# Decoder layer stack on one core: odd heads' sums taken from the exponentials, cross scores in two steps, a new order of work

## The chip, the cores and the metric

The kernel runs on one core of a Trainium2 chip, in one launch. The metric is the device time of that core in microseconds, as a median over runs. The core has five engines that run side by side: PE (TensorE, the matrix products and transpositions), DVE (VectorE), ACT (ScalarE, which computes the exponentials), POOL (GpSimd) and SP (SyncE, which here only issues transfers). They meet at semaphores. PE writes its results into PSUM, in banks of 128 x 512 numbers, and PE cannot reuse a bank before ACT or DVE has read it.

## What is computed

There are 4 sequences of 512 tokens with 128 channels. Three blocks follow each other, each with a residual sum and a layer norm: a retention attention with 16 heads, a cross attention to 32 keys for each sequence, and a stack of six layers of local attention (16 heads of 64, windows of 32 that look at themselves and the window before) and a gated FFN. Cut to what matters here:

```python
def local_attention(q, k, v):
    ...
    sim = jnp.einsum('bhwie,bhwje->bhwij', bq, bk2) * QK_SCALE
    sim = jnp.where(mask, -jnp.finfo(sim.dtype).max, sim)
    attn = jax.nn.softmax(sim, -1)
    out = jnp.einsum('bhwij,bhwje->bhwie', attn, bv2)
...
def _L0_xattn_ref(key, value, query, mask, inv_scale_factor, W1, b1, W2, b2, W3):
    q = jnp.einsum('bqd,hd->bqh', query, W1) + b1
    k = jnp.einsum('bkd,hd->bkh', key, W2) + b2
    qk = jnp.einsum('bqh,bkh->bqk', q, k) / inv_scale_factor
    attn = jax.nn.softmax(qk, axis=-1)
...
for i in range(DEPTH):      # 6
    x = attn_layer(shift_tokens(x), Wqkv[i], q_scale[i], k_scale[i], Wo[i]) + x
    x = ffn_layer(shift_tokens(x), ln_g[i], ln_b[i], W1[i], b1[i], W2[i], b2[i]) + x
```

## The kernel before

**An order written out ahead.** The kernel first records all its work as steps and only then emits it. A step (`Step`, recorded by `Work.do` at line 328) belongs to one engine and has a planned cost in us, a function that issues its instructions, the slots that it reads and writes, and a priority. A slot is a tile to be: a place in an SBUF pool or a PSUM bank. `Plan.order` (line 180) plays the steps through: an engine that is free takes, among the waiting steps that find room for their slots, the one with the lowest priority; on PE it may pass over up to `KEEP` = 4.5 units of priority to avoid a dear turn from one kind of work to another (`TURN`, `TURNS`, lines 143 to 148). A step is over after its planned cost; those that read from it may start `LAG` = 0.25 us later, and the slots that it was last to use are free again at its planned end (lines 228 to 232). The list that comes out is the order of instructions on every engine, SP's transfers too. The chip then runs each engine in exactly this order, with semaphores wherever one engine needs another. The planned costs thus never appear as times on the chip; they only decide who stands before whom.

A priority is a base (the number of the unit of work), an offset, and a correction from the table `SHIFT` (lines 294 to 317), whose keys are a group letter and the number of the step in its group: P for a pair of heads of the first block, X for cross attention, u for a unit of the layers, q for its values, f for the FFN, w, v, k for weights. `ROOM` (line 286) says how many places each slot kind has: three PSUM banks `mm`, two `tr`, two `so`, one `f`; a bank asked for as `mm` may also come from the other pools.

**Front.** Lines 394 to 1030: for each sequence eight pairs of heads (`pair`), then `finish` (residual, norm) and `cross`. `cross` (line 977) makes the scores of a sequence in one step on PE (`scores`, lines 987 to 992): for each of four blocks of 128 tokens a product of x with the folded keys and a product of a row of ones with the bias row, both added up in PSUM. One DVE step then takes the maximum, ACT the exponentials, DVE the shares.

**Layers.** For each layer, sequence, half of the heads (8) and block of 128 tokens there is a unit: 6 x 4 x 2 x 4 = 192 of them (`unit`, line 1209, and `attend`, line 1335). A unit has these steps, by the lines that the profile shows:

- PE: two projections pq and pk, each a product of three passes (`mm3`, lines 87 to 89)
- ACT: squares sq (1258). DVE: rotary products t1 and t2 (1242, 1251), norms (1275, 1282). POOL: their sum (1264)
- ACT and POOL: inverse norms r, u (1345 to 1352); POOL scales t1 by r (1362)
- PE: transpositions ptq and ptk (96). ACT: copies into qT and kT (1385). POOL: the window before (1397)
- PE: scores of 8 heads (1408, 1421), even heads into the bank s0, odd heads into s1
- DVE: maxima mx of both (1441), and even heads' scores minus maximum (1450)
- ACT: for the odd heads four exponentials of 64 columns each, with the maximum as bias (`exps`, 1460); for the even heads one exponential over all four (1463)
- DVE: sums su of all 8 heads (1466) and their inverse (1467). POOL: weights times inverse sums (1473)
- PE: transposition pp (1483). ACT: copy pT (1487)
- PE: output O of 32 small products (1499), which also needs the values vb

Every two units share the values: four products pv (PE), four copies v (ACT, 1306), and twelve transfers on SP that lay v out by windows in vb (1313 to 1325). vb has two places, so its transfers wait until O of two pairs before has read it. After the four blocks of both halves come `add_attention` (1510) and `ffn` (1534), whose second product is pyf (1625).

The matters around the change: the bank s1 goes to the exponentials in `exps` and is free after them; `su` has three places; `total` (lines 1465 to 1469) is one DVE step of two instructions.

## Time and profile before

| | us |
|---|---|
| median of 3 runs | 2003.3 (2001.99 to 2007.96) |
| the profiled execution | 2008.77 |
| its span | 2007.1 |

The span is the time between the first and the last instruction of the profile; the 1.7 us to the execution's time lie around it. The mean granted clock of TensorE was 0.976. By the timeline, the first block and most of cross attention take the first 360 us, the first scores of a layer begin at 409.0 us and the last at 1973 us. The first O of the six layers begins at 423, 707, 969, 1229, 1486 and 1744 us.

Some groups of the layers, with the mean of one instruction as recorded:

| line, engine | instruction | count | busy us | mean ns |
|---|---|---|---|---|
| L1264 POOL | t1q, t1k sum, 128x512 | 384 | 500.0 | 1302 |
| L1362 POOL | t1q, t1k times r, 128x512 | 384 | 402.1 | 1050 |
| L1275 DVE | norms, 128x1024 | 192 | 231.8 | 1207 |
| L1306 ACT | copy v, 128x512 | 384 | 219.8 | 602 |
| L1473 POOL | weights times inverse sums, 128x512 | 192 | 204.2 | 1068 |
| L1463 ACT | even heads' exponential, 128x256 | 192 | 81.0 | 436 |
| L1450 DVE | even heads' scores minus maximum, 128x256 | 192 | 76.7 | 409 |
| L1467 DVE | inverse of the sums, 128x8 | 192 | 39.0 | 203 |
| L1586, L1587 ACT | table loads around the FFN's gelu | 25 + 25 | 64.2 | 1283 |
| L989, L990 PE | cross scores, x part and bias part, 32 columns | 32 + 32 | 14.5 | 308, 313 |

How to read it: a record lasts from the start of an instruction to its end, and the next one may start before that, on every engine. So records add up to more than the engine needs; the distance from one start to the next is the price of an instruction in a row of others. A matrix product of 32-bit numbers appears as two records. The waits of an engine name what released it last.

### The profile page before, as it was taken

How to read it: one execution, taken by the hardware profiler on the slowest of the kernel's cores; microseconds unless marked ns; L12 is line 12 of the kernel's file. 1: busy time of each engine (PE TensorE's matmuls, PEld its weight loads, DVE VectorE, ACT ScalarE, POOL GpSimd, SP SyncE). 2: the span in 40 equal slices, each digit the busy share in tenths (PEclk: the TensorE clock that was granted, in tenths of full speed). 3: DMA queues.
4: the chain of work that ended last, by engine and by line, in shares of the span. 5: the costliest groups of instructions: out<-in, count | busy, mean ns of one | idle time of the engine just before them, and what ended most of it. 6: DMA issues, size and time to landing. Idle time of an engine off the chain costs nothing.

```text
span 2007.1 us, 71083 instructions
## 1 busy us (share of the span) xinstructions
PE 1850.5 (92%) x28633; PEld 1405.3 (70%) x28633; DVE 1611.1 (80%) x3482; ACT 1587.4 (79%) x4048; POOL 1441.8 (72%) x1847
## 2 busy tenths in 40 slices
PE   7999999788898999989999999999999998999996
PEld 5676677566676777767777777777777776767675
DVE  5787786757787798886998868989788897888885
ACT  7877765689887788878888888888878897788785
POOL 3444444666777688886887878878878888787882
PEclk9999997789999999999999999999999999999999
DMA  3000001254555565665555555656655565545662
GB/s 90 1 6 2 1 2 34 67 130 109 133 148 123 131 152 139 156 150 147 133 132 146 146 146 142 166 123 160 150 142 144 125 157 149 142 107 134 146 172 60
DMA packets 146464, 233.02 MB, mean 116 GB/s; under 512 B 23770, under 2 KB 39000, under 8 KB 146136
## 3 DMA queue, kind: packets, MB, share of 16 engines
q1 hardware_dynamic: 146136, 228.46, 45.7%
q8 instruction: 228, 3.74, 0.8%
q14 instruction: 100, 0.82, 0.1%
HBM read 31.25 MB, written 2.10 MB: 17 GB/s over the span
## 4 chain that ended last, share of the span: by engine, by line
PE 57%; ACT 18%; DVE 14%; DMA 4%; issue 3%; SPq 3%; POOL 1%; DVEq 0%; ACTq 0%; POOLq 0%
PE O L1499 6%; PE s L1421 4%; PE pv L87 4%; DMA vb<-v 4%; PE pv L89 3%; PE pv L88 3%; PE ptk L96 3%; PE pp L1483 3%; PE ptq L96 2%; SPq L1325 2%; PE pyf L1625 2%; DVE nx L1275 2%; ACT sq L1258 2%; ACT v L1306 2%; PE pq L87 1%
## 5 line engine op out<-in xcount | busy, mean ns | idle before, releaser
L1264 POOL TENSOR_TENSOR t1q<-t1q,t2q 128x512 f32<-128x512 f32 x192 | 248.7, 1295 | 66.4 <-DVE t2q L1251 62.6
L1264 POOL TENSOR_TENSOR t1k<-t1k,t2k 128x512 f32<-128x512 f32 x192 | 251.3, 1310 | 55.4 <-DVE t2k L1251 40.7
L1473 POOL TENSOR_TENSOR pr<-pr,su 128x512 f32<-128x512 f32 x192 | 204.2, 1068 | 91.0 <-DVE su L1467 73.7
L1306 ACT COPY v<-pv 128x512 f32<-128x512 f32 x384 | 219.8, 602 | 42.7 <-PE pv L89 37.4
L1275 DVE TENSOR_REDUCE nx<-sq 128x16 f32<-128x1024 f32 x192 | 231.8, 1207 | 4.9 <-ACT sq L1258 3.7
L1499 PE MATMUL O<-vb,pT 128*32 128x128 f32 x6144 | 210.9, 279 | 10.5 <-DMA vb<-v 4.8
L1499 PEld LDWEIGHTS O<-vb,pT 128*32 128x32 f32 x6144 | 165.0, 111 | 63.3 <-issue 30.3
L1362 POOL TENSOR_TENSOR t1q<-t1q,r 128x512 f32<-128x512 f32 x192 | 201.2, 1051 | 2.7
L1362 POOL TENSOR_TENSOR t1k<-t1k,r 128x512 f32<-128x512 f32 x192 | 200.9, 1049 | 0.0
L1421 PE MATMUL s<-kT,qT 64*32 64x64 f32 x12288 | 169.8, 223 | 22.6 <-issue 22.5
L1460 ACT ACTIVATE pr<-s,mx 128x64 f32<-128x64 f32 x768 | 178.2, 325 | 9.8 <-DVE mx L1441 9.8
L1441 DVE TENSOR_REDUCE mx<-s 128x4 f32<-128x256 f32 x384 | 145.6, 413 | 42.7 <-PE s L1421 41.3
L1242 DVE TENSOR_TENSOR t1k<-pk,tl 128x512 f32<-128x512 f32 x192 | 130.7, 681 | 56.0 <-PE pk L89 34.8
L1242 DVE TENSOR_TENSOR t1q<-pq,tl 128x512 f32<-128x512 f32 x192 | 130.7, 681 | 50.7 <-PE pq L89 37.0
L1421 PEld LDWEIGHTS s<-kT,qT 64*32 64x32 f32 x12288 | 151.0, 105 | 25.0 <-issue 24.5
L1258 ACT ACTIVATE sq<-pk 128x512 f32<-128x512 f32 x192 | 116.1, 610 | 41.6 <-DVE t1k L1242 23.9
L1251 DVE TENSOR_TENSOR t2q<-pq,tl 128x512 f32<-128x512 f32 x192 | 130.0, 677 | 21.0 <-ACT sq L1258 20.1
L1466 DVE TENSOR_REDUCE su<-pr 128x8 f32<-128x512 f32 x192 | 129.3, 673 | 20.8 <-ACT pr L1463 12.0
L1251 DVE TENSOR_TENSOR t2k<-pk,tl 128x512 f32<-128x512 f32 x192 | 130.4, 679 | 18.8 <-ACT sq L1258 18.6
L1487 ACT COPY pT<-pp 128x512 f32<-128x512 f32 x192 | 113.3, 596 | 24.3 <-PE pp L1483 23.1
L1258 ACT ACTIVATE sq<-pq 128x512 f32<-128x512 f32 x192 | 115.6, 614 | 20.9 <-DVE t1q L1242 18.2
L96 PE MATMUL ptq<-ident,t1q 128*128 128x128 f32 x768 | 120.0, 280 | 11.6 <-DVE t2k L1251 4.6
(1002 smaller groups left out, 5428.3 us busy)
## 6 DMA issues: line engine op xcount, KB each, us to landing
vb<-v SPq DMA_DIRECT2D x576, 256.0 KB
vb<-v SPq DMA_DIRECT2D x192, 128.0 KB
vb<-v SPq DMA_DIRECT2D x288, 64.0 KB
vb<-in_c_zero_dram SPq DMA_DIRECT2D x96, 64.0 KB
wo<-in_L_ffn_Wo_dram SPq DMA_DIRECT2D x12, 256.0 KB
tb<-in_c_tabs_dram SPq DMA_DIRECT2D x12, 256.0 KB
w1r<-in_L_ffn_W_dram SPq DMA_DIRECT2D x6, 341.0 KB
xt<-in_x_dram SPq DMA_DIRECT2D x4, 256.0 KB
```

The source lines that it names most:

```text
L96: self.nc.tensor.transpose(bank[: blk.shape[1], tslice(t)], blk, self.ident)
L1242: nc.vector.tensor_tensor(out=t1(), in0=ps().rearrange("p (h d) -> p h d", d=DH), in1=tl()[:, 2 * j, t : t + 1, :].to_broadcast([P, 8, DH] ...
L1251: nc.vector.tensor_tensor(out=t2().rearrange("p h (z d) -> p h z d", z=2), in0=ps().rearrange("p (h z d) -> p h z d", d=32, z=2)[:, :, ::- ...
L1258: do("ACT", self.A512, lambda ps=ps, j=j: nc.scalar.activation(sq()[:, j], ps(), AF.Square), [ps], [sq])
L1264: lambda t1=t1, t2=t2: nc.gpsimd.tensor_tensor(out=t1(), in0=t1(), in1=t2(), op=ALU.add),
L1275: nc.vector.tensor_reduce(out=near()[:, :, 0], in_=sq().rearrange("p j (h d) -> p (j h) d", d=DH), op=ALU.add, axis=AX.X,)
L1306: do("ACT", self.A512, lambda pv=pv, j=j, e=e: nc.scalar.copy(v()[:, j, e], pv()), [pv], [v])
L1362: lambda x=x, j=j: nc.gpsimd.tensor_tensor(out=x(), in0=x(), in1=r()[:, j].unsqueeze(2).to_broadcast([P, 8, DH]), op=ALU.mult),
L1421: nc.tensor.matmul(sv[e]()[rows, p, :], lhsT=qT()[c, p, rows], rhs=kT()[c, p, 32 * w : 32 * w + 64], start=False, stop=True, skip_group_ch ...
L1460: nc.scalar.activation(pr()[:, a, 1], sv[1]()[:, a], AF.Exp, bias=mx()[:, a, 1:2])
L1473: lambda: nc.gpsimd.tensor_tensor(out=flat(), in0=flat(), in1=su().unsqueeze(2).to_broadcast([P, 8, 64]), op=ALU.mult),
L1499: nc.tensor.matmul(o[rows, t], lhsT=pT()[:, p, rows], rhs=vb()[:, t % 2, w, tslice(p)], start=(h2 == t == p == 0), stop=(h2 == 1 and p == ...
```

## The change

Four parts. In `exps`, each of the four exponentials also delivers the sum of its 64 columns (`accum_out`) into an odd column of `su`; `total` then sums only the even heads (128 x 256 instead of 128 x 512) before it takes the inverses. In `cross`, the scores are two steps of two blocks each; a step first writes the bias for both blocks with one product and then adds the two products of x. In the plan, a slot that becomes free is given out `GIVE` = 0.2 us after the planned end of its last user instead of at once, `TURNS` has other prices, some planned costs are different, and the planned time of a weight's load is 11 us instead of 8. The table `SHIFT` has new numbers throughout, so the order of steps on all engines is another one. Nothing else of what is computed is changed.

```diff
+    GIVE = 0.2
+
     TURN = 0.04
     TURNS = {
-        ("t", "t"): 0.08, ("t", None): 0.0, (None, "t"): 0.0, ("t", "S"): 0.17, ("t", "O"): 0.17, (None, "S"): 0.09,
-        (None, "O"): 0.09, ("S", "t"): 0.17, ("S", None): 0.17, ("S", "O"): 0.27, ("S", "f"): 0.17,
-        ("O", "t"): 0.0, ("O", None): 0.0, ("O", "S"): 0.0, ("O", "f"): 0.0, ("t", "f"): 0.08,
+        ("t", "t"): 0.08, ("t", None): 0.0, (None, "t"): 0.06, ("t", "S"): 0.17, ("t", "O"): 0.17, (None, "S"): 0.12,
+        (None, "O"): 0.12, ("S", "t"): 0.2, ("S", None): 0.19, ("S", "O"): 0.19, ("S", "f"): 0.17,
+        ("O", "t"): 0.1, ("O", None): 0.1, ("O", "S"): 0.09, ("O", "f"): 0.1, ("t", "f"): 0.08, ("f", "O"): 0.2,
     }
...
+                if over == 2:
+                    for g in st.freed:
+                        free[g] += 1
+                    continue
                 busy.discard(st.eng)
+                st.freed = []
                 for s in st.slots:
                     left[s] -= 1
                     if left[s] == 0 and s.tags:
-                        free[s.got] += 1
+                        st.freed.append(s.got)
+                if st.freed:
+                    heapq.heappush(events, (now + self.GIVE, st.n, 2, st))
...
     SHIFT = dict(
-        C1=5.5, C2=8.5, C3=-2.75, D0=19.5, D2=12.75, D3=-11.25, D4=-0.5, D6=3.25, D7=12.25, D8=-1.25, D9=-7.75,
...
+        C0=-7, C2=1.5, C3=-6.75, D0=11, D1=-7.75, D2=-0.75, D4=13.5, D5=9.25, D6=1.25, D7=-11.75, D8=-8.5,
...
-    PE3, PE_T, PE_S, PE_AV = 0.73, 0.37, 0.72, 1.01
+    PE3, PE_T, PE_S, PE_AV = 0.72, 0.36, 0.7, 0.91
...
-    DMA = 8.0
+    DMA = 11.0
...
-        def scores():
-            for t in range(NT):
-                nc.tensor.matmul(view()[:, t, :], lhsT=x[:, tslice(t)], rhs=M[:, keys], start=True, stop=False)
-                nc.tensor.matmul(view()[:, t, :], lhsT=unit, rhs=br[:, keys], start=False, stop=True)
-
-        do("PE", 2.7, scores, [X, bs], [pq], kind="g")
+        def scores(t):
+            two = br[:, keys].unsqueeze(1).to_broadcast([1, 2, SK])
+            nc.tensor.matmul(view()[:, t : t + 2, :], lhsT=unit, rhs=two, start=True, stop=False, skip_group_check=True)
+            for j in range(t, t + 2):
+                nc.tensor.matmul(
+                    view()[:, j, :], lhsT=x[:, tslice(j)], rhs=M[:, keys], start=False, stop=True, skip_group_check=True
+                )
+
+        for t in (0, 2):
+            do("PE", 0.9, lambda t=t: scores(t), [X, bs], [pq], kind="g")
...
-            self.do("PE", 0.85, prod, [wt, wo], [ps])
+            self.do("PE", 1.05, prod, [wt, wo], [ps])
...
-                nc.scalar.activation(pr()[:, a, 1], sv[1]()[:, a], AF.Exp, bias=mx()[:, a, 1:2])
-
-        do("ACT", 0.82, exps, [mx, s[1]], [parts[1]], hold=[pr])
+                nc.scalar.activation(
+                    pr()[:, a, 1], sv[1]()[:, a], AF.Exp, bias=mx()[:, a, 1:2], accum_out=su()[:, 2 * a + 1 : 2 * a + 2]
+                )
+
+        do("ACT", 0.9, exps, [mx, s[1]], [parts[1]], hold=[pr, su])
...
-            nc.vector.tensor_reduce(out=su(), in_=flat(), op=ALU.add, axis=AX.X)
+            nc.vector.tensor_reduce(out=su()[:, 0:8:2], in_=pr()[:, :, 0], op=ALU.add, axis=AX.X)
             nc.vector.reciprocal(su(), su())
 
-        do("DVE", 0.84, total, parts, [su], hold=[pr])
+        do("DVE", 0.6, total, parts, [su], hold=[pr])
```

## The prediction

> **What bounds the kernel now.** I read the page's busy line first, then the same engines stage by stage, then the order of work on PE in the timeline.
>
> ```profile
> span 2007.1 us, 71083 instructions
> PE 1850.5 (92%) x28633; PEld 1405.3 (70%) x28633; DVE 1611.1 (80%) x3482; ACT 1587.4 (79%) x4048; POOL 1441.8 (72%) x1847
> ...
> PE 57%; ACT 18%; DVE 14%; DMA 4%; issue 3%; SPq 3%; POOL 1%; DVEq 0%; ACTq 0%; POOLq 0%
> ```
>
> ```profile
> core 0: us, PE busy (x) PEld busy (x) DVE busy (x) ACT busy (x) POOL busy (x), PEclk, DMA share, GB/s
> 0.00:300.00 300.00, 277.51 (x2356) 203.33 (x2356) 222.44 (x579) 223.34 (x537) 133.23 (x160) 0.98 0.06 17
> 300.00:560.00 260.00, 222.34 (x2776) 167.30 (x2776) 188.45 (x437) 195.39 (x432) 165.57 (x211) 0.87 0.36 91
> 560.00:1950.00 1390.00, 1310.00 (x22842) 1004.16 (x22845) 1165.53 (x2372) 1135.38 (x3003) 1123.67 (x1451) 1.00 0.58 144
> ```
>
> No engine is idle for long. Over the six layers (the third row) PE is 94% busy, DVE 84, ACT 82, POOL 81. PE records overlap, so I took PE's work from starts instead: I cut PE's stream into groups and took the time from one group's first matmul to the next one's. The groups are p (a product of three), t (four transposes), S (scores of one unit), O (output of one unit) and f (the FFN's second product). These lines show it:
>
> ```profile
> 1066.53 0.60 PE L96 MATMUL ptq<-ident,t1q 128*128 128x128 f32 x4
> 1066.96 0.60 PE L1483 MATMUL pp<-ident,pr 128*128 128x128 f32 x4
> 1067.32 0.47 PE L87 MATMUL phf<-xhf,w1h 128*114 128x512 f32 x1
> ...
> 1068.45 0.48 PE L87 MATMUL pq<-wq21h,yh 128*128 128x512 f32 x1
> ...
> 1069.32 1.95 PE L1499 MATMUL O<-vb,pT 128*32 128x128 f32 x64
> 1071.20 0.30 PE L1408 MATMUL s<-msk,identb 64*32 64x256 bf16 x8
> 1071.32 0.84 PE L1421 MATMUL s<-kT,qT 64*32 64x64 f32 x64
> 1072.10 0.48 PE L87 MATMUL phf<-xhf,w1h 128*114 128x512 f32 x1
> ```
>
> A transposition costs 0.43 us before another one (1066.53 to 1066.96) and 0.36 before a product; a product before O costs 0.87; two O groups and the turn to S take 1.88; S before a product takes 0.90. The lower quartile of every pair of kinds between 560 and 1950 us is PE's price without waits. Summed, it falls 163 us short of that stretch. So PE's own work is some 1227 of 1390 us (88%), and 163 us are waits. Of these, 129 us are in 224 waits of over 0.12 us. By what released each one, I put 83 us in 150 waits down to a PSUM bank that an ACT or DVE instruction had just finished reading (a transposition held back by t2k, a product by pr, the scores by sq), 29 us to data, and 16 us stay unnamed. The kernel is bound by PE's work plus small waits for the other engines, 0.55 us each.
>
> **The parts.** Unless said otherwise, a pitch is the lower quartile of starts in the timeline between 560 and 1950 us.
>
> *The odd heads' sums.* These rows carry it:
>
> ```profile
> L1460 ACT ACTIVATE pr<-s,mx 128x64 f32<-128x64 f32 x768 | 178.2, 325 | 9.8 <-DVE mx L1441 9.8
> L1441 DVE TENSOR_REDUCE mx<-s 128x4 f32<-128x256 f32 x384 | 145.6, 413 | 42.7 <-PE s L1421 41.3
> L1466 DVE TENSOR_REDUCE su<-pr 128x8 f32<-128x512 f32 x192 | 129.3, 673 | 20.8 <-ACT pr L1463 12.0
> L1345 ACT ACTIVATE r<-n 128x16 f32<-128x16 f32 x192 | 43.2, 225 | 49.7 <-DVE n L1282 49.3
> L1347 ACT ACTIVATE u<-r 128x16 f32<-128x16 f32 x192 | 41.5, 216 | 12.0 <-ACT r L1346 0.4
> ```
>
> DVE: 192 reductions shrink from 128x512 to 128x256. The nearest row of that size is mx: 413 instead of 673 ns, so 0.26 x 192 = 50 us. The other bound, from pitches (708 for su, 331 for mx), is 0.38 x 192 = 72 us. I take 50. DVE does not bound, so this is worth nothing by itself; it makes the chain from scores to weights 0.26 us shorter.
>
> ACT: 768 exponentials also deliver a sum. No instruction before does that. Their pitch is 196 ns (four in a row and on to the next instruction take 787). Lower bound: nothing, since the sum rides along. Upper bound: one more ACT instruction each that waits for its predecessor, as L1345 does before L1346: a pitch of 247 ns, 190 us in all. In between is a short instruction that waits for nothing, 122 ns (L1347): 94 us. I take 0.12 each, as reading a finished sum resembles that row most. ACT then goes from 1587 to about 1681 us. Within the layers its own pitches sum to 1076 of 1390 us; 677 of the exponentials lie there, so it becomes 1076 + 83 = 1159, still below PE's 1227. The cover is this idle quarter of ACT. A unit's chain pays 4 x 0.12 - 0.26 = +0.2 us between scores and weights, and the new plan gives it no more room: counted in the built order with these prices of PE, the median distance from the scores to the transposition of the weights goes from 6.8 to 6.4 us of PE work.
>
> [...]
>
> The plan allows only 0.90 - 0.82 = 0.08 us for the four sums. By my price the ACT instructions behind come 0.4 us later than planned. Behind them stand copies (kT, qT, pT, v) that free banks for PE: 109 of the 224 waits are released by ACT. If a third of these grow by 0.4 us, that is 36 x 0.4 = +14 us; bounds 0 (free sums) and +44 (all of them).
>
> *Cross scores.* Per batch, four bias products become two wide ones, in two steps instead of one. The profile has 32 + 32 records of 0.31 us for four batches; 16 go, at most 5 us if they stood alone. Between them other work can now run. I take -2 (bounds 0 and -5). They run between 294 and 430 us.
>
> *Turns on PE.* Same groups, another order; the built programs let me count neighbours. Over the pure p, t, S, O and f neighbours of the whole program (before, after; dearer than the cheapest successor by): p-t 374, 299 (0.08); t-t 130, 239 (0.08); t-S 58, 24 (0.175); t-O 40, 53 (0.175); p-S 36, 17 (0.095); p-O 91, 83 (0.097); S to anything else 142, 136 (0.205); O to p or t 108, 63 (0.114); O-S 49, 96 (0.09); f-O 11, 0 (0.196). The sums are 118 and 110 us: -8 us.
>
> *The plan's rule for banks.* A freed slot is now given out 0.2 us after the last reader's end. Steps that would have waited that long on the chip are planned elsewhere. At 0.2 us for each of the 150 bank waits that is -30 us in the layers (bounds 0 and -83, all of them). In the same order the median distance from the transposition of q and k to the scores grows from 2.5 to 5.8 us of PE work, which covers the ACT copy between (0.6 us) and the bank. It falls from 17.9 to 15.6 us at the lower quartile for the values' transfers (counted from the freed buffer and the last value product, whichever is later, to the first O). SP still issues 12 transfers for a pair of units, 10 us in a row of the timeline (1199.8 to 1210.1), and 1284 in the whole program, as before; what is late when they are late is O. I price that at +2 (bounds 0 and the case D below).
>
> *The passage into the layers.* From 300 to 560 us the granted clock is 0.87 and PE 86% busy; in the new order the first q product again follows the last pairs, at PE work 439 against 437 us. The plan now counts 11 us for a weight's load instead of 8, so PE's 2.8 us wait for the first folded values (wvt) may go. ACT gets two more table loads (93 for 91, 1.28 us each), which its idle quarter hides; without that cover +3. I price the passage at nothing, with +-10 us if the gaps there move the clock.
>
> **The sum.** +14 - 2 - 8 - 30 + 2 = -24 us. On the profiled execution (2008.8 us, its span 2007.1) this gives 1985; the median of the runs is 5.5 lower, 2003.3, so 1979.
>
> **The rivals.**
> *A, the forecast:* small waits shrink, the sums are hidden: 1955 to 1994, 1979. For it: half of PE's waits are bank waits. Against it: waits this short can reappear elsewhere. 0.62.
> *B, the new order only exchanges waits:* turns -8, cross -2, sums +14 and no bank wait saved: 2007; with free sums 1993. It speaks for B that all five engines are 80% loaded or more and one order's repaired wait is another's new one. Middle 2000. 0.17, of which 0.08 within the bound, 0.06 faster, 0.03 slower.
> *C, the sums make ACT the bound:* place: the four exponentials of each unit. From 0.22 us each ACT's layer work (1076 + 677 x 0.22 = 1225) reaches PE's 1227, and from there each further tenth counts in full. At the upper bound (0.247) it is 1243. At PE's share of the stretch (0.88) the layers take 1243 / 0.88 = 1413, +23, and the bank gain is gone: 2003 + 23 - 10 = 2016; with all the waits for ACT grown as well (+44), 2060. Against it: 0.12 us is nearer to the short rows. 0.14, slower.
> *D, the values' transfers come late:* the chain of waits already has 4% DMA and 3% SP. With 2.3 us less room in 96 pairs, at a third of the pairs it costs 32 x 2.3 = +74, less the 24 saved: 2053. Against it: only 4.8 us of PE's idle time are put down to these transfers. 0.07, of which 0.06 slower and 0.01 within the bound.
>
> **How the numbers follow.** From 0.3% (6 us) a measurement of this kernel tells a change from none. Faster: 0.62 (A) + 0.06 (B) = 0.68; same: 0.08 (B) + 0.01 (D) = 0.09; slower: 0.03 (B) + 0.14 (C) + 0.06 (D) = 0.23. The range reaches from A with two thirds of the bank waits gone (-55 for -30: 1954, less 4) to C's middle: 1950 to 2026; A's own is 1955 to 1994.
>
> **What would show it.** Right: L1466's successor near 0.41 us, exponentials' groups of four near 1.3 us, the time from 560 on shorter by about 25 us, the number of bank waits down, PE's share of the layers up by one to two points. Wrong: ACT over 92% in the layers (C), O released by DMA far more often (D), waits of the same sum behind other instructions (B), or four exponentials still at 0.8 us, which takes away the +14 and the case C with it.

## The result, and the profile after

| | us |
|---|---|
| before, median in this sitting | 2005.63 (2001.99 to 2011.99) |
| after, median of 4 runs | 2055.76 (2054.04 to 2065.67) |
| ratio, with its 95% interval | 1.0257 (1.0213 to 1.0300) |
| the profiled execution after | 2056.45, its span 2054.7 |

The changed kernel is 2.6% slower. The forecast was 1979 us, with a range of 1950 to 2026; the time lies outside it, on the other side. The busy line and the summary of the chain of waits of the changed kernel:

```profile
span 2054.7 us, 71723 instructions
PE 1850.0 (90%) x28617; PEld 1415.4 (69%) x28617; DVE 1572.2 (77%) x3482; ACT 1648.9 (80%) x4818; POOL 1435.1 (70%) x1847
...
PE 51%; ACT 21%; DVE 16%; issue 5%; DMA 3%; SPq 1%; POOL 0%; ACTq 0%; DVEq 0%; POOLq 0%
```

PE does the same work (1850 us against 1850.5) in a span that is 47.6 us longer, so its share falls from 92 to 90%. ACT grows by 61.5 us and has 770 more instructions, DVE shrinks by 39 us. In the chain, ACT rises from 18 to 21% and "issue" from 3 to 5%: time in which an engine waited for nothing that the profile shows. The same three stages as before, busy time of each engine and, behind the engines, the granted clock:

```profile
core 0: us, PE busy (x) PEld busy (x) DVE busy (x) ACT busy (x) POOL busy (x), PEclk, DMA share, GB/s
0.00:300.00 300.00, 277.36 (x2290) 204.03 (x2290) 216.05 (x561) 217.32 (x522) 127.49 (x152) 0.95 0.07 17
300.00:560.00 260.00, 213.65 (x2772) 157.54 (x2773) 188.78 (x436) 203.77 (x502) 167.16 (x216) 0.89 0.36 87
560.00:1950.00 1390.00, 1272.84 (x22092) 988.27 (x22097) 1095.55 (x2301) 1152.53 (x3578) 1082.88 (x1403) 0.98 0.59 140
```

In the first two rows little changes, and the first O of the layers begins at 426 us against 423. The loss is in the third row: PE is 91.6% busy instead of 94.2%, and runs 22,092 of its instructions in these 1390 us instead of 22,842. The first O of the six layers now begins at 426, 709, 976, 1241, 1517 and 1790 us: from the second layer on the distances are 267, 265, 276 and 273 us, where they were 261, 260, 258 and 257. So it is no single place, and the later layers lose more: 6, 5, 18 and 15 us.

What the changed instructions cost is seen in these groups of the changed kernel, busy us and mean ns of one:

```profile
L1472 ACT ACTIVATE pr<-s,mx 128x64 f32<-128x64 f32 x768 | 230.0, 318 | 43.1 <-DVE mx L1453 42.9
L1472 ACT ACTIVATION_READ_ACCUMULATOR pr<-s,mx 128x1 f32 x768 | 162.2, 211 | 0.0
L1480 DVE TENSOR_REDUCE su<-pr 128x4 f32<-128x256 f32 x192 | 79.2, 413 | 31.0 <-ACT pr L1477 29.4
```

The sum that rides along is a second ACT instruction for each exponential, 768 of them. The timeline of ACT for one unit shows what they cost in a row:

```profile
642.38 0.32 ACT L1472 ACTIVATE pr<-s,mx 128x64 f32<-128x64 f32 x1
642.59 0.20 ACT L1472 ACTIVATION_READ_ACCUMULATOR pr<-s,mx 128x1 f32 x1
642.68 0.32 ACT L1472 ACTIVATE pr<-s,mx 128x64 f32<-128x64 f32 x1
...
643.46 0.22 ACT L1472 ACTIVATION_READ_ACCUMULATOR pr<-s,mx 128x1 f32 x1
643.55 0.44 ACT L1477 ACTIVATE pr<-pr 128x256 f32<-128x256 f32 x1
```

A reading takes 0.09 us from its start to the next start (642.59 to 642.68), and four exponentials with their sums 1.17 us here (642.38 to 643.55), 1.155 in the lower quartile over all units; without the sums that was 0.787. That is 0.37 us for a unit, where the new plan allows 0.08. DVE's reduction takes 413 ns.

For the layers I then took the time in which PE runs neither a product nor a weight load, from 420 us to the end. It is 106.5 us before and 156.4 us after, in 228 gaps each. The sizes differ most at two places: gaps of 0.2 to 1 us fall from 115 (56.8 us) to 85 (42.6 us), while gaps of 2 to 3 us rise from 5 (11.5 us) to 25 (59.1 us). What released PE at the end of such gaps, first before, then after (total us, times, longest):

```profile
PE s L1421 <- issue: 22.5, 26, 2.3
PE s L1408 <- ACT qT L1385: 7.8, 12, 1.5
...
PE ptq L96 <- DVE t2k L1251: 4.6, 9, 1.0
```

```profile
PE s L1433 <- issue: 58.8, 38, 3.7
PE phf L87 <- ACT pT L1501: 17.7, 9, 2.2
PE pv L87 <- ACT pr L1472: 5.6, 10, 2.3
```

The small waits of before for qT and t2k are gone (one of 1.5 us for qT is left). In their place stand gaps inside the scores, between one product and the next, that no engine ends; and gaps before the FFN's first product (phf). The timeline of the changed kernel has one of each:

```profile
1256.17 0.56 PE L1433 MATMUL s<-kT,qT 64*32 64x64 f32 x28
1259.43 0.60 PE L1433 MATMUL s<-kT,qT 64*32 64x64 f32 x36 [2.70 <-issue]
```

```profile
1201.43 0.40 PE L89 MATMUL pv<-wv30h,yl 128*128 128x512 f32 x1
1203.98 0.48 PE L87 MATMUL phf<-xhf,w1h 128*114 128x512 f32 x1 [2.15 <-ACT pT L1501]
```

In the first, 28 of the 64 product records of a unit's scores have run, their operands have been there from the first one on, and PE stands still for 2.70 us. In the second, phf needs the bank that ACT's copy pT reads, and ACT's timeline shows why the copy is late:

```profile
1199.06 1.28 ACT L1600 ACT_TABLE_LOAD   x1
1200.35 1.67 ACT L1600 ACTIVATE hidf<-hidf 114x512 f32<-114x512 f32 x3
1202.04 1.28 ACT L1601 ACT_TABLE_LOAD   x1
1203.34 0.59 ACT L1501 COPY pT<-pp 128x512 f32<-128x512 f32 x1
```

The copy is queued behind a gelu with its two table loads, 4.2 us in all.

A third thing is in the clock. From 420 us on, the granted clock is at one half for 38.9 us before and for 79.4 us after. Of the 36 gaps over 1.5 us in the changed kernel, 18 are followed by such a stretch within 12 us of their beginning (8 of 13 before). The trace has a price for it: a product before another product takes 1.28 us inside such stretches and 0.69 outside (lower quartiles). The groups of PE's work that lie wholly inside them took 49 us in the changed kernel, 21 us more than the same pairs of groups at full clock (in the median); before it was 19 us, 8 us more. At that rate the 40.5 us more at half the clock are worth an estimated 17 us.

These three readings (50 us more idle time, some 17 us of clock, 6 to 8 us of turns saved) add up to some 60 us, more than the 47.6, and none of them says yet whether the sums or the order bring them about.

### The profile page after: what moved, and what is told of

It is laid out like the page before. It is cut to its first block, busy times and chain, and to the rows that moved or that the text cites. A ratio compares the mean times of both kernels' runs of the same rounds, so it can differ in the third digit from the quotient of the medians.

```text
span 2054.7 us, 71723 instructions
## 1 busy us (share of the span) xinstructions
PE 1850.0 (90%) x28617; PEld 1415.4 (69%) x28617; DVE 1572.2 (77%) x3482; ACT 1648.9 (80%) x4818; POOL 1435.1 (70%) x1847
## 4 chain that ended last, share of the span: by engine, by line
PE 51%; ACT 21%; DVE 16%; issue 5%; DMA 3%; SPq 1%; POOL 0%; ACTq 0%; DVEq 0%; POOLq 0%
PE O L1513 6%; PE s L1433 4%; PE pv L87 3%; ACT pr L1472 3%; PE pyf L1639 3%; ACT sq L1270 3%; PE pv L89 3%; PE pv L88 3%; PE pp L1497 3%; DMA vb<-v 3%; DVE nx L1287 2%; PE ptq L96 2%; ACT v L1318 2%; PE ptk L96 2%; PE phf L87 1%
## 5 line engine op out<-in xcount | busy, mean ns | idle before, releaser
L1276 POOL TENSOR_TENSOR t1k<-t1k,t2k 128x512 f32<-128x512 f32 x192 | 246.4, 1287 | 52.4 <-DVE t1k L1254 41.4
L1472 ACT ACTIVATE pr<-s,mx 128x64 f32<-128x64 f32 x768 | 230.0, 318 | 43.1 <-DVE mx L1453 42.9
L1433 PE MATMUL s<-kT,qT 64*32 64x64 f32 x12288 | 171.4, 227 | 59.5 <-issue 58.8
L1513 PE MATMUL O<-vb,pT 128*32 128x128 f32 x6144 | 215.4, 280 | 6.4 <-ACT pT L1501 3.0
L1513 PEld LDWEIGHTS O<-vb,pT 128*32 128x32 f32 x6144 | 169.2, 112 | 51.6 <-issue 20.1
L1472 ACT ACTIVATION_READ_ACCUMULATOR pr<-s,mx 128x1 f32 x768 | 162.2, 211 | 0.0
L96 PE MATMUL ptq<-ident,t1q 128*128 128x128 f32 x768 | 120.2, 280 | 11.5 <-DVE t2q L1263 3.9
L1397 ACT COPY kT<-ptk 128x512 f32<-128x512 f32 x192 | 117.8, 619 | 15.4 <-PE ptk L96 15.3
```

Source lines behind the costliest of these rows:

```text
L96: self.nc.tensor.transpose(bank[: blk.shape[1], tslice(t)], blk, self.ident)
L1276: lambda t1=t1, t2=t2: nc.gpsimd.tensor_tensor(out=t1(), in0=t1(), in1=t2(), op=ALU.add),
L1433: nc.tensor.matmul(sv[e]()[rows, p, :], lhsT=qT()[c, p, rows], rhs=kT()[c, p, 32 * w : 32 * w + 64], start=False, stop=True, skip_group_ch ...
L1472: nc.scalar.activation(pr()[:, a, 1], sv[1]()[:, a], AF.Exp, bias=mx()[:, a, 1:2], accum_out=su()[:, 2 * a + 1 : 2 * a + 2])
L1513: nc.tensor.matmul(o[rows, t], lhsT=pT()[:, p, rows], rhs=vb()[:, t % 2, w, tslice(p)], start=(h2 == t == p == 0), stop=(h2 == 1 and p == ...
```

## The experiments

**Which part of the change costs the time?** Theory S puts the loss down to the sums on ACT, theory O to the new order. Four kernels hold one part fixed: each has exactly the order of one parent and the sums of the other, or no sums of the odd heads at all.

e1, the changed kernel in its order, with the sums of before:

```diff
-                nc.scalar.activation(
-                    pr()[:, a, 1], sv[1]()[:, a], AF.Exp, bias=mx()[:, a, 1:2], accum_out=su()[:, 2 * a + 1 : 2 * a + 2]
-                )
+                nc.scalar.activation(pr()[:, a, 1], sv[1]()[:, a], AF.Exp, bias=mx()[:, a, 1:2])
...
-            nc.vector.tensor_reduce(out=su()[:, 0:8:2], in_=pr()[:, :, 0], op=ALU.add, axis=AX.X)
+            nc.vector.tensor_reduce(out=su(), in_=flat(), op=ALU.add, axis=AX.X)
```

> The changed kernel, every engine's order kept to the instruction, with the sums as before: no accumulators, DVE reduces 128x512. Theory S (the sums: 768 accumulator reads of 92 ns pitch put 0.37 us on ACT per unit, where the plan allowed 0.08): the reads go, DVE gets 0.26 us per unit that the plan doesn't know; 1980 to 2015. Theory O (the new order is slow by itself): 2050 or more, as the reads were not the matter and DVE gets more work.

e2, the kernel before in its order, with the new sums (the same lines the other way round, and su held by the step of the exponentials):

> The kernel before, every engine's order kept to the instruction, with the new sums: accumulators in the four exponentials, DVE reduces 128x256. S: ACT gets 0.37 us per unit that this plan doesn't know either, 192 x 0.37 = 71 us of which a third to all shows: 2025 to 2055. O: ACT's idle quarter hides it: 2000 to 2012.

e3 and e4, the new and the old order with the halved reduction and without any sum on ACT. The odd heads' sums are left out; their weights are multiplied by the even heads' inverse sums, in an instruction of the same size:

```diff
-            nc.vector.reciprocal(su(), su())
+            nc.vector.reciprocal(su()[:, 0:8:2], su()[:, 0:8:2])
...
-                out=flat(), in0=flat(), in1=su().unsqueeze(2).to_broadcast([P, 8, 64]), op=ALU.mult
+                out=pr(),
+                in0=pr(),
+                in1=su().rearrange("p (a e) -> p a e", e=2)[:, :, 0:1].unsqueeze(3).to_broadcast([P, 4, 2, 64]),
+                op=ALU.mult,
```

> The changed kernel's order with sums that cost nothing: no accumulators, DVE sums the even heads only and the odd heads' weights are multiplied by the even heads' inverse sums (the odd heads' sums are left out). What the plan assumed, within 0.08 us per unit. S: 1970 to 1990, the gain that was planned. O: 2030 or more.

> The order before with sums that cost nothing (the odd heads' sums are left out, as in the run beside it). It shows what 0.26 us less of DVE per unit is worth where the order doesn't count on it. S and O both: 1990 to 2005, since DVE doesn't bound; with the run beside it this gives the price of the order alone.

Measured, as ratios to before with their 95% intervals:

| | sums as before | sums from the exponentials | odd heads' sums left out |
|---|---|---|---|
| order before | 1 | 1.0134 (1.0090 to 1.0179), 2029 us | 0.9979 (0.9961 to 0.9997), 1997 us |
| new order | 1.0249 (1.0217 to 1.0280), 2050 us | 1.0257 (1.0213 to 1.0300), 2056 us | 1.0190 (1.0161 to 1.0220), 2040 us |

The rows differ by 1.2 to 2.5% whatever the sums are, so the order is the larger cause: with the sums of before, the new order costs 2.5% (49 us against the 2001.5 us of before in that sitting). S falls as the account of the loss (e1 and e3 lie above its ranges), though not everywhere: e2 lies in its range and above O's. The new order's row also holds the cross scores in two steps, but no loss comes from there: at the first O of the second layer e1 is not behind yet (704.9 us against 707.3). The columns show the rest. In the old order the accumulators cost 1.3% (28 us; 32 against no odd sums at all), in the new order hardly anything against DVE's sums (0.1%, within the intervals) and 0.7%, some 13 us, against none. The two parts do not add: 28 and 49 would be 77, and the change costs 50. The smaller reduction by itself is worth 0.2%.

The gaps of the changed kernel come with the order too. PE's waits from 420 us on, first in e1 and then in e2:

```profile
PE s L1433 <- issue: 54.7, 37, 3.4
PE phf L87 <- ACT pT L1499: 17.4, 9, 2.2
```

```profile
PE s L1421 <- issue: 22.3, 24, 2.5
```

e1, without a sum on ACT, has the two groups of gaps of the changed kernel; e2, with the odd heads' sums on ACT, has the gaps inside the scores of the kernel before.

How the accumulators cost 28 us in the old order is seen in PE's waits over 0.12 us between 560 and 1950 us, taken as in the prediction: those released by ACT go from 109 with 64.8 us to 150 with 85.4 us (+20.6). That is the wait that the prediction named, for copies behind the exponentials.

**Are the gaps inside the scores a lack of instructions?** Scores are dense: 144 instructions (weight loads counted) in 0.69 us. An output has 64 in 0.90 (16 products, two records and two weight loads each), a product of three 6 in 0.69. In the new order dense groups stand together more often: an output directly ahead of scores 96 times instead of 49. The gaps inside the scores without a releaser (those over 0.3 us: 24 before, 35 after) ended 1.4 us in the median after a packet of 16,384 bytes had ended on the instruction queue (0.8 to 1.7). Theory I: PE has run out of instructions and waits for the next packet. Theory B: these gaps are waits for banks or data that the profile fails to name. In e5 to e8 a function sorts the finished order once more: `spread` pulls a later sparse PE step (a product or a transposition that depends on nothing between) up between dense ones, `early` pulls ACT's copies up ahead of a gelu.

```diff
-            for st in plan.order():
+            out = plan.order()
+            marks(out)
+            for st in spread(out, 2, 8, 150):
                 st.fn()
```

e5 is the changed kernel with 223 steps moved so, e6 the changed kernel with ACT steps moved ahead of 19 of 25 gelus (`early(out, 2, 4)`), e7 both, e8 the kernel before with 137 steps moved.

> The changed kernel; on PE alone, 223 sparse groups (products, transpositions) that nothing holds back are moved up, each between two dense groups (scores: 144 instructions, O: 64) that stood side by side; the other engines keep their order. Theory I (PE runs out of instructions where scores and O stand together: the gaps inside scores that no engine releases end 1.4 us after an instruction packet, 35 such gaps and 59 us of issue wait in the changed kernel, 24 and 23 us in the one before): the gaps go to under 25, issue wait inside scores to under 30 us, fewer half clock windows, at about 20 us of dearer turns: 2015 to 2045. Theory B (only the planned waits for banks count): the gaps stay, the turns are paid: 2055 to 2080.

> The changed kernel; at 19 of the 25 gelu steps (table load, three gelus, table load: 4.2 us of ACT) one or two ACT steps from behind are moved ahead of them, so that the banks that they read come free; nothing else is moved. Theory B: the eight waits of 2.15 us of phf for a copy of pT behind the gelu go, with the half clock window that follows each: 2025 to 2045. Theory I: 2045 to 2060.

> Both edits on the changed kernel. If both theories hold, their gains add up: 1995 to 2025. If only one does, like that one alone.

> The kernel before with the same spreading on PE (137 sparse groups between dense ones). I: its 24 gaps inside scores halve, -15 to -20 us, against 18 us of dearer turns: 1985 to 2010. B: 2010 to 2025.

| | ratio (95%) | us | gaps inside scores, us | all idle time of PE from 420 us | half clock | turns |
|---|---|---|---|---|---|---|
| before | 1 | 2004 | 22.5 | 106.5 | 38.9 | 101 |
| after | 1.0257 | 2056 | 58.8 | 156.4 | 79.4 | 95 |
| e5 | 1.0496 (1.0476 to 1.0516) | 2105 | 12.4 | 156.5 | 76.0 | 118 |
| e6 | 1.0277 (1.0256 to 1.0298) | 2061 | 52.2 | 151.2 | 97.3 | 95 |
| e7 | 1.0461 (1.0432 to 1.0491) | 2096 | 9.5 | 148.5 | 63.5 | 118 |
| e8 | 1.0209 (1.0185 to 1.0234) | 2048 | 6.3 | 114.8 | 43.0 | 118 |

(Turns: the prediction's prices, summed over the neighbours from the layers' first output to the last.) The gaps behave as I says: spread the dense steps, and they go from 58.8 to 12.4 us and from 22.5 to 6.3. The time does not follow: both orders become slower, by 49 and 43 us, and e5, e7 and e8 lie above the ranges of both theories. 23 and 17 us of that are dearer turns, and the idle time is as long as before or longer, in other places. In e5 products now wait for a bank that DVE reads:

```profile
PE phf L87 <- ACT pT L1501: 17.7, 9, 2.2
PE s L1433 <- issue: 12.4, 13, 2.1
PE pq L87 <- DVE pr L1462: 8.1, 6, 1.9
PE pv L87 <- DVE pr L1462: 6.3, 13, 1.0
```

In the changed kernel five of the eight waits of phf have a half clock window behind them, begun within 1 us of the wait's end; the expectation for e6 put one behind each. In e6 the line of phf and pT is gone from the list, and in its place stands a wait for v; the time is no shorter:

```profile
PE s L1433 <- issue: 52.2, 34, 3.8
PE s L1420 <- ACT v L1318: 9.6, 8, 1.4
PE pv L87 <- ACT pr L1472: 6.8, 13, 2.3
```

Neither source of gaps could be removed by moving single steps without a price elsewhere. This left two questions: whether I holds apart from the kernel, and whether a smaller dose gains.

**The groups by themselves.** e9 is the kernel before, followed by groups of the layers' shapes on constants, with nothing to wait for and nothing that uses them.

```diff
             for st in plan.order():
                 st.fn()
+            Alone(k).run()
...
+        for n in range(24):
+            self.score()
...
+        for n in range(24):
+            self.output()
...
+        for n in range(12):
+            self.output()
+            self.output()
+            self.score()
+            self.score()
...
+        for n in range(24):
+            self.score()
+            self.product()
+            self.product()
```

> The kernel before, followed by work that nothing uses: groups of the layers' shapes on constants, with nothing to wait for (24 scores in a row; 24 outputs in a row; 12 times two outputs and two scores; 24 times a score and two products; 24 products of three between the parts). Theory I (PE runs out of instructions where dense groups stand together): gaps of PE that no engine releases appear in the parts of dense groups alone, of 2 to 3 us, about one for each two or three groups of scores (16384-byte packets at 144 instructions a group), so that a score costs well over the 0.69 us that it takes in the layers, on average 1.0 us or more, and the parts with two products between the scores have none (0.69 + 2 x 0.69 + turns of 0.3, 2.4 us each). Theory B (the gaps inside scores are waits for banks or data that the profile fails to name): no part has a gap over 0.5 us, since nothing is waited for here; 24 scores take 24 x 0.69 = 16.6 us and 24 outputs 24 x 0.90 = 21.6 us.

The windows of the four parts in e9, in this order:

```profile
2009.96:2050.40 40.44, 23.89 (x1440) 21.01 (x1441) 0.00 (x0) 0.00 (x0) 0.00 (x0) 0.56 0.02 4
2068.76:2090.16 21.40, 21.36 (x769) 20.74 (x769) 0.00 (x0) 0.00 (x0) 0.00 (x0) 1.00 0.02 5
2105.80:2172.48 66.68, 46.58 (x2497) 39.73 (x2497) 0.00 (x0) 0.00 (x0) 0.00 (x0) 0.97 0.02 5
2188.24:2242.80 54.56, 54.03 (x1867) 31.00 (x1859) 0.00 (x0) 0.00 (x0) 0.00 (x0) 1.00 0.02 4
```

24 scores in a row take 40.4 us, 1.69 each; in the layers one takes 0.69. PE is busy in 59% of that time though nothing holds it. 24 outputs in a row run without a gap, 0.89 each. Two outputs and two scores take 66.7 / 12 = 5.56 us where their prices and turns make 3.5. With two products behind each score the gaps are all but gone (one of 0.53 us in 24): 2.27 us a round. (The products here are 16-bit ones of the same tile, three in a row.) The timeline of the first part shows the rhythm:

```profile
2010.77 0.71 PE L1730 MATMUL alone<-ident 64*32 64x64 f32 x48
2013.71 0.35 PE L1730 MATMUL alone<-ident 64*32 64x64 f32 x16 [2.23 <-issue]
...
2014.65 0.67 PE L1730 MATMUL alone<-ident 64*32 64x64 f32 x32
2017.45 0.68 PE L1730 MATMUL alone<-ident 64*32 64x64 f32 x32 [2.13 <-issue]
```

From 2009.96 to 2049.79 the gaps end every 3.47 or 3.75 us, and from each of these ends to the next PE starts exactly 256 products and weight loads, twelve times over. That is one packet: e9 has 14,448 more instructions than the kernel before and 56 more packets of 16,384 bytes, 258 each. The lines show that a gap can fall anywhere inside a group. In the third part the gaps come in the same rhythm, 256 or 512 instructions apart and 3.47 to 3.76 us for each 256, at a granted clock of 0.97; so the half clock is not what makes it. The parts without gaps fit as well: 256 instructions of outputs alone take 3.57 us, of a score with two products 3.73. So I is shown where nothing else runs: PE gets 256 of these short instructions in some 3.6 us once it has used up what was there.

The layers show the same mark. Counted over all of PE's instructions in the program (waits and other instructions of its sequencer included), every one of the 24 gaps before, and of the 35 in the changed kernel, ends a whole number of 256 instructions after the others (22.0 and 58.0 us in all). The gaps that another engine ends are spread over all places of the count. So these gaps are the want of instructions in the layers too, and theory B's reading of them falls.

The clock falls here without any wait for another engine: it is granted at one half from 2015.0 to 2055.9 us, begun where PE does nothing but these scores and stands still between them. The products behind show that it is real: they start 0.427 us apart until then and 0.216 us afterwards. In the third part, with gaps of 0.5 to 2.0 us and PE busy 70% of the time instead of 59%, the clock is at one half for 3.4 us only.

**A smaller dose, and another order from the old plan.** e10 and e11 move a step only where more than 290 instructions of dense groups would stand in a row (`spread(out, 1, 8, 290)`): 49 steps in the new order, 29 in the old. e13 gives the old planner a little more freedom on PE, which yields another order from the same table:

```diff
-    KEEP = 4.5
+    KEEP = 5.0
```

> The changed kernel with 49 sparse PE groups (instead of 223) moved between dense ones, only where more than 290 instructions of dense groups would stand in a row. Theory I, with the loss of the first spreading put down to its many turns and moved waits: the gaps without a releaser inside the scores fall from 58.8 to about 30 us, the turns cost some 5 us instead of 23, and the time falls below the changed kernel's, to 2030 to 2050 us. Theory B (these gaps only stand for waits that appear elsewhere once they are gone): 2056 us or more, 2060 to 2075, with the idle time of PE unchanged near 156 us.

> The kernel before with 29 sparse PE groups (instead of 137) moved between dense ones by the same rule. Theory I: of the 22.5 us of gaps inside the scores about half go, for some 3 us of turns: 1990 to 2000 us, faster than before by up to 0.5%. Theory B: 2005 to 2020 us, as the hand-made moves only put waits elsewhere.

> The kernel before, its planner allowed to pass over 5.0 units of priority on PE instead of 4.5, all else as before: another order from the same table. The planner's own total for it is 1851.3 us against 1809.9 (+41.4), and for the changed kernel's order 1824.1 by the same rules (+14.2). Theory P (the planner's total by the old rules, scaled by 2003/1810, tells the time on the chip): +41.4 x 1.107 = +46, 2049 us, and the changed order's +14 would be 2019, so that most of its +45 is not in the plan. Theory R (the order before is a find that suits the chip in ways that no plan tells, and any other order of this kernel loses some 2%): 2040 to 2055 as well, but then e14-like orders with any total do. Theory N (orders with fewer dense groups in a row are better on the chip whatever the plan says; this one has 17 stretches of 256 instructions that would take under 2.6 us against 26 before and 31 in the changed kernel): under 2030 us, with gaps inside the scores below 20 us.

| | ratio (95%) | us | gaps inside scores | all idle time | half clock | turns |
|---|---|---|---|---|---|---|
| e10 | 1.0300 (1.0252 to 1.0347) | 2059 | 35.1 | 144.2 | 62.7 | 107 |
| e11 | 1.0082 (1.0055 to 1.0109) | 2018 | 18.0 | 105.5 | 59.7 | 107 |
| e13 | 1.0316 (1.0261 to 1.0372) | 2062 | 11.0 | 137.7 | 66.6 | 105 |

In e10, 24 us of gaps inside the scores go, but only 12 us of idle time, and the turns take 12 back: no gain. Theory I had 2030 to 2050 here and is wrong on what its gaps are worth. In e11 the idle time stays, the turns cost 6 us and the clock is at half for 21 us more: 15 us slower. Both times lie where theory B had them (2056 or more; 2005 to 2020). e13 was the surprise. It has few gaps inside the scores (11.0 us), fewer stretches of dense groups than before, no accumulators, and is still 3.2% slower. Theory N, that dense stretches decide, falls with it. What is longer are other waits of PE (from 420 to 2000 us):

```profile
PE phf L87 <- ACT pT L1487: 11.7, 8, 2.7
PE s L1421 <- issue: 11.0, 12, 2.4
PE O L1499 <- ACT pT L1487: 9.1, 5, 3.0
PE O L1499 <- DMA vb<-v: 7.4, 5, 2.3
```

So the order before is not one of many equal ones. The planner knows that: by its own rules its total is 1809.9 us for the order before and 1851.3 for e13's.

**Does the planner's total tell the time?** Two more orders answer this, whose totals lie well above those of their parents: e12, the kernel before with `LAG = 0.27` for 0.25, and e14, the changed kernel with `GIVE = 0.0` for 0.2, which takes the new rule for freed slots back.

> The kernel before, its planner letting a reader start 0.27 us after its writer's planned end instead of 0.25: another order from the same table. By the old rules of the planner its order takes 1869.5 us, against 1809.9 for the order before, 1824.1 for the changed kernel's and 1851.3 for that of the last experiment, which took 2062 us on the chip. Theory P (the planner's total tells the time): longer than that one by 18.2 x 2003/1810 = 20 us, 2082 (2072 to 2095). Theory R (only the order before suits the chip, all others lie near 2.5% above it whatever their total): 2045 to 2065.

> The changed kernel, its planner giving out freed slots at once (0.0 instead of 0.2 us): the new rule for banks alone taken back, with the same table, so another order. By the new rules without the 0.2 us its order takes 1870.7 us, the changed kernel's 1831.6. Theory P: 39 x 2003/1810 = 43 us slower than the changed kernel, 2097 (2085 to 2110). Theory R: no worse than the changed kernel by more than 10 us, 2045 to 2065. If my rule of 0.2 us for each bank wait held on the chip, bank waits would come back here: some 30 us on top of either.

| order | total by the old rules, us | over before | measured ratio (95%) | us over before |
|---|---|---|---|---|
| before | 1809.9 | | 1 | |
| e13 | 1851.3 | 41 | 1.0316 (1.0261 to 1.0372) | 60 |
| e12 | 1869.5 | 60 | 1.0382 (1.0337 to 1.0428) | 75 |
| after | 1824.1 | 14 | 1.0257 (1.0213 to 1.0300) | 50 |
| e14 | 1862.0 | 52 | 1.0675 (1.0633 to 1.0716) | 135 |

(The total of a finished order: each engine takes its steps in that order, with the old turns, no time for freed slots, and the kernel's own planned costs.) e12 took 2080.1 us where theory P had 2082; R (2045 to 2065) falls. e14 took 2139.9, beyond both theories: it is worse than the changed kernel by 84 us where P has 43. From 420 us on it has 48 us of gaps inside the scores (58.8 in the changed kernel), 26 us of PE's waits released by POOL against 3, and the clock at half for 152 us. And 25 of the 84 us are lost ahead of the layers: their first O begins at 450.5 us instead of 425.5. Its bank waits, counted as in the prediction, are 162 with 108 us, against 171 with 103 us in the changed kernel: the 30 us of bank waits that my rule would bring back did not come, although P with these 30 on top (2115 to 2140) would fit the time. So the totals put orders of one planner in the right sequence (before, e13, e12; after, e14), and the chip makes the distances from the parent larger. Between the planners they put the new order 14 us behind the old one, not ahead; by the new rules (new turns, 0.2 us for freed slots) the same replay gives 1898.1 us for the old order and 1836.6 for the new one, a gain of 61 us that the chip turns into a loss of 50.

**Gaps taken away by the plan.** Moving steps by hand pays in turns and in other waits. e15 lets the order be found with the gaps in the sum: the kernel before, its planner untouched, with another table.

```diff
     SHIFT = dict(
-        C1=5.5, C2=8.5, C3=-2.75, D0=19.5, D2=12.75, D3=-11.25, D4=-0.5, D6=3.25, D7=12.25, D8=-1.25, D9=-7.75,
...
+        C0=-1.25, C1=7, C2=7.75, C3=-1.5, D0=19.25, D1=2.75, D2=5, D3=-2.75, D4=-0.5, D5=-9, D6=1.75, D7=14,
...
```

225 numbers differ, by random steps, each kept if the finished order's sum did not grow. Besides the turns and 3.6 us for 256 instructions, the sum lets a reader start 0.35 us after its writer's end and a bank be used 0.1 us after its last reader's (two assumed values).

> The kernel before, all planner rules as before, with another table of corrections (SHIFT), found by small random steps from the old one. A step was kept when the finished order, added up with the prices measured in these runs, became shorter: the turns as in the prediction, and 3.6 us for each further 256 PE instructions once the last are used up, as the groups by themselves showed. By the planner's own rules the total hardly moves (1806.5 for 1809.9 us); by the measured prices it falls from 1903.3 to 1887.0 us (-16.3), of which gaps for want of instructions 47.7 to 29.9. For the changed kernel's order that sum is 1923.0 (+19.7). Theory I, in the form that gaps inside the scores cost time and come back only if the whole order is planned for it: faster than before, -10 to -25 us (1978 to 1993), with the gaps inside the scores at half of their 22.5 us or less. Theory P (the planner's own total tells): -3.4 x 1.1 = -4 us, within 0.3%. Theory B or R (any order but the old one loses, gaps come back as other waits): 2020 us or more.

Measured: 1983.7 us, ratio 0.9877 (0.9849 to 0.9906), 23.5 us faster than before. Stages and largest waits of PE in e15, which computes all that the reference asks for:

```profile
560.00:1950.00 1390.00, 1328.54 (x23262) 1006.07 (x23260) 1181.60 (x2403) 1151.99 (x3050) 1133.88 (x1460) 1.00 0.59 145
```

```profile
PE s L1421 <- issue: 10.8, 14, 1.3
PE s L1408 <- ACT qT L1385: 5.0, 7, 1.5
PE pv L87 <- DVE X L1647: 3.9, 5, 0.9
```

PE is 95.6% busy in the layers (94.2 before, 91.6 after). Its idle time falls from 106.5 to 84.9 us, the gaps inside the scores from 22.5 to 10.8, although the turns cost 108 us instead of 101; the half clock is where it was (39.2 us). The planner's own total (P: -4 us) did not tell this, and R and B fall: another order can win. By the same sum the changed kernel's order is 19.7 us behind that of before, of which 12 are gaps for want of instructions (59.7 for 47.7); without a price for these it would be 6.4 behind (1868.8 against 1862.4). The chip made 49 of it, so the sum tells the sign and less than half of the size. e15 was not separated into its parts: bank waits fell in it too, from 150 with 83 us to 124 with 62 us, so its gain does not show what the gaps for want of instructions are worth.

## Why the prediction was wrong

*The bound.* PE was named rightly. Its groups cost in the new order what they cost in the old one: the lower quartile of a transposition before a product is 0.355 us in both, of scores before scores 0.685, of an output before scores 0.99 to 1.01.

*DVE's reduction:* 413 ns, as taken, and worth little by itself (0.2%, e4).

*ACT's sums:* each is a second instruction on ACT: the changed kernel has the record ACTIVATION_READ_ACCUMULATOR 768 times, the kernel before not once. Price 0.092 us from its start to the next instead of the 0.12 taken. The mechanism of the term held (copies behind the exponentials come late). Its size depends on the order: 28 us in the old one, and in the new one, for which +14 was taken, 0.1% against DVE's sums and some 13 us against none; all within the bounds 0 to 44. ACT does not become the bound (case C): it is 83% busy in the layers and e1, without the sums, is as slow as the changed kernel.

*Turns and cross scores:* the turns are 6 us cheaper in the layers of the built order, by the prices of the prediction. The passage into the layers is where it was (first O at 426 against 423); the +-10 us for its clock were the author's estimate, and the granted clock there is 0.89 against 0.87. Neither matters for the result.

*The values' transfers (case D):* no. O waits 2.0 us for these transfers in the changed kernel, where it waited 4.8.

*The step that failed is the rule for banks, -30.* "Steps that would have waited that long on the chip are planned elsewhere": they are, and the short waits did shrink (gaps of 0.2 to 1 us by 14 us, the named waits for qT and t2k away). But the bank waits as a class did not go: 150 with 83 us became 171 with 103 us. Two things were wrong in it. First, the bounds, "0 and -83", allowed no loss, and the range had no room for one of this size either: its upper end, "C's middle: 2026", does not follow from the 2016 and 2060 that C itself gives. The term priced one difference between the orders and took all others at nothing, although the order was planned anew from the first step to the last. e1 shows that the order, without a changed instruction in the layers' sums, costs 2.5%, 49 us. Second, the two gaps that grew were in reach of the profile of before and of the built order. The profile had the line of gaps inside the scores without a releaser (22.5 us, 26 times); it grew to 58.8 us. The prediction counted outputs ahead of scores, 49 to 96, priced them as a cheap turn of 0.09 us, and left unnamed waits at 16 us without asking what they were. And phf behind a gelu stands in the built order: its bank's reader comes after two table loads (17.7 us).

*Case B* ("the new order only exchanges waits") was the nearest, with the right sentence in it: one order's repaired wait is another's new one. It was given a middle of 2000 us and a share of 0.03 for slower, because it took an exchange to be even. By the runs it is not: of the other orders that were not searched for with prices of the chip, from two planners or sorted by hand, the best lost 0.8%.

*What stays open.* What grew in the new order (36 us of gaps inside the scores, 17 us of phf, an estimated 17 us of half clock, less 14 us of short waits and 6 us of turns) makes some 50 us. The runs do not show that these parts are the loss: other gaps that grew are left out, and all idle time with the clock and the turns makes 60. And no run gives back a part of it in that order by removing one source alone: e5, e6, e7 and e10 removed them and paid elsewhere, and e15, where planning them away paid, starts from the old order and lost bank waits as well. So the sources are shown, their shares of the 50 us are not. Which part of the new plan made the order slow (the 0.2 us for freed slots, the prices or the table) is open as well: e14 takes the 0.2 us back and is slower still, but its table had been made for them. e14's excess over its total wasn't followed up beyond the 25 us ahead of the layers.

## What to carry to other kernels

Where a change comes with a new order of the whole program, the order can be the largest part of the change, as it was here, and it can have either sign: take the two finished orders, add up each whole with one set of prices measured on the chip, instead of pricing one rule of the planner, and let the range hold a loss of the size by which other orders of the same kernel differ (here 1 to 7%). A wait in the profile that nothing releases is a cause to be found before the forecast, not a remainder: a search with a price for the want of instructions in its sum, among others, found the one complete kernel here that beats both (1.2% faster than before). And single steps moved by hand in a tight order gave back here what they saved, or more; in e15 the planner with another table kept it.

## What the runs showed of the hardware

*Instructions run out.* In e9 PE is bound by the supply of instructions: 24 groups of scores without any wait take 1.69 us each, where one takes 0.69 in the layers, with a gap each 3.47 to 3.75 us, one packet of 256 instructions apart, which is some 14 ns an instruction. With two products of three after each group, one gap of 0.53 us is left in 24 rounds. In the layers all 24 unnamed gaps inside the scores before, and all 35 after, stand whole blocks of 256 instructions apart.

*The clock and PE's gaps.* In e9 the clock goes to one half for 41 us while PE runs scores with gaps of 1.2 to 2.2 us and nothing else (PE busy 59% of that part, no gap over 2.23 us), and is full again 5.5 us after the products behind them have begun; with PE busy 70% of the time, in the third part, it does so for 3.4 us only. In the kernels themselves gaps over 1.5 us are followed by a stretch at half the clock in about half of the cases (8 of 13 before, 18 of 36 after). These stretches come in units of 3.41 us: from 420 us on each lasts 3.41 or 6.83 us, but for the one that the end of the record cuts off.

*In the changed kernel an accumulator that is written out is its own instruction on ACT*: 768 records of 0.211 us, at 0.092 us in a row.
